# First convolution of a four-layer graph network: its first block ahead of all others, rows of x loaded in the third block, scores copied out of records by GpSimd

## The chip, the cores and the metric

The kernel runs on one core of one Trainium2 chip. The metric is the device time of one execution in microseconds (us), as the median of several runs. Lower is better. The core has five engines: TensorE (PE; PEld is its weight load), VectorE (DVE), ScalarE (ACT), GpSimd (POOL) and SyncE (SP), which only issues transfers. ACT and POOL issue transfers too, from the same in-order streams in which their computations stand.

## The reference

3125 nodes with 256 features x, 100,000 edges (src, dst) with 128 attributes and two weights each. Four graph layers follow one another; each adds its result to x and normalizes the rows.

```
edge_index = stack([src, dst])
x = layernorm(x + L0(x, edge_index, W1, W2))              # two graph convolutions
x = layernorm(x + L1(x, edge_index, edge_attr_128, ...))  # attention over edges
x = layernorm(x + L2(x, src, dst, edge_weight, ...))      # gated step, sums both ways
x = layernorm(x + L3(x, edge_index, W_conv, ...))         # convolution and decoder
```

The change lies in L0. With self-loops added to the edges, and deg the number of edges that end in a node:

```
gcn_conv(x, W): h = x @ W;  dinv = rsqrt(deg)
                return segment_sum(h[src] * (dinv[src] * dinv[dst])[:, None], dst)
L0(x) = gcn_conv(relu(gcn_conv(x, W1)), W2)
```

The score of an edge in L1 is a sum of a part from its source node and a part from its attributes. The latter, called q here, depends on the inputs alone.

## The kernel before

**Blocks and slabs.** The nodes lie in 25 blocks of 128 rows (`NBK`, `P`). Between two blocks lies a 128x128 count matrix; the 25 such matrices that end in one target block are its slab. A convolution is, for each target block, 75 matrix products that accumulate into one bank: 25 source blocks times three bf16 parts of each float32 feature (`apply_parts`, line 769, result `acc`).

**First stage (0 to 1041 us).** Chunks of 16 edges per partition are sorted into a table in device memory: a rank is computed for each edge, and POOL scatters its record (packed row numbers, the two weights, q) by an indirect transfer, 784 in all (line 498, `table`). ACT and DVE meanwhile make `H0`, the three bf16 parts of x @ W1 times dinv. The last of these parts come from lines 341 (ACT) and 343 (DVE, named `features` in the profile). The order of PE, DVE, ACT and SP in this stage is written out by hand (`manual_schedule`).

**First convolution (1041 to 1344 us).** This is the loop `for b in range(NBK)` from line 822. For each target block b:

- `load_records(b)`: SP loads the 50 columns of records of this block (line 803, `rec_b`, three buffers); it waits for all scatters. DVE unpacks the row numbers into `keys` and `keyd` (lines 807 to 814, five instructions), and ACT copies field 3 of the records into `q` (line 815).
- For the two halves of the slab (13 and 12 source blocks), DVE makes one-hot matrices: `os`, 128 columns, and `od`, 64 columns (line 723; two buffers each).
- `build_slab`: PE multiplies them (line 749, `slab`, three buffers, four source blocks in each), and ACT copies each group into the slab (line 750, `wo`, four buffers). The block's own matrix gets the identity on top, for the self-loops.
- SP stores the slab for later layers (line 829), PE applies it to `H0` (line 769), ACT applies relu and scale (line 832), PE turns the result and multiplies it with W2 (lines 680 and 687), and ACT and DVE split the product into three bf16 parts, `H1` (lines 706 to 710).

**What else is loaded here.** The rows of x, 3.2 MB, are issued by ACT at line 657, ahead of the loop. W2 is loaded by ACT ahead of the loop (line 820, through `weight`, line 666). The attention layer's `WnT`, `bn` and `attn_r` are loaded by ACT behind the loop in the text (lines 850 and 851; issues at lines 666 and 671). x is first read in the loop behind this one (line 877, the second convolution), WnT, bn and attn_r there as well.

**What sets the order.** Outside the first stage a planner orders the instructions of each engine. It ranks them by their place in the text, takes those that are ready by its own estimate of times, and so mixes stages and blocks: issues that stand behind the loop in the text can be placed ahead of it, and records of several blocks are loaded and unpacked far ahead. Each engine then runs its instructions strictly in that order. Line 648 adds a dependence by hand: `up` (line 647) comes behind the last of the parts (line 343).

**A second path** (`general_path`), for graphs that don't fit the slabs, stands behind a flag and doesn't run with these inputs.

Of the kernel before, what the change touches and what calls it, by code (L numbers as in the profile page):

```python
# [8 lines left out]
F32 = mybir.dt.float32  # L9
BF = mybir.dt.bfloat16  # L10
I32 = mybir.dt.int32
AF = mybir.ActivationFunctionType
# [6 lines left out]
P = 128  # L19
# [7 lines left out]
def row_bcast(vec, parts=P):  # L27

    return bass.AP(tensor=vec.tensor, offset=vec.offset, ap=[[0, parts], [1, vec.shape[0]]])
# [8 lines left out]
NBK = 25  # L38
# [3 lines left out]
TB = 2  # L42
HP = 64
# [9 lines left out]
KD = ND // P  # L53
# [46 lines left out]
def dense_path(ctx: ExitStack, tc: tile.TileContext, a: dict, out: bass.AP, flag: bass.AP):  # L100
    nc = tc.nc
    N, D = 3125, ND
# [548 lines left out]
    keyd = keep.tile([P, NT, 2], BF, name="keyd")  # L651
    keys = keep.tile([P, NT, 2], BF, name="keys")
# [1 line left out]
    nc.gpsimd.memset(x1[:, :, 0], 1.0)  # L654
    nc.gpsimd.memset(x1[:, :, D + 1], 1.0)
    x = x1[:, :, 1:D + 1]
    nc.scalar.dma_start(x, a["x_rows"])
    stats = keep.tile([P, NBK, 2], F32, name="stats")
    rstd = keep.tile([P, NBK], F32, name="rstd")
    s1 = keep.tile([P, NBK], F32, name="s1")  # L660


    def weight(pool, v, name):
        k, m = v.shape
        t = pool.tile([P, k // P, m], F32, name=name)
        nc.scalar.dma_start(t, v.rearrange("(k p) m -> p k m", p=P))
        return t

    def bias(pool, v, name):
        t = pool.tile([P, v.shape[0]], F32, name=name)  # L670
        nc.scalar.dma_start(t, row_bcast(v))
        return t
# [31 lines left out]
    def split(dst, src, shape):  # L704

        nc.scalar.activation(dst[0], src, AF.Copy)  # L706
        r = wk.tile(shape, F32, name="split")
        nc.vector.tensor_tensor(r, src, dst[0], op=OP.subtract)
        nc.scalar.activation(dst[1], r, AF.Copy)
        nc.vector.tensor_tensor(dst[2], r, dst[1], op=OP.subtract)  # L710
# [3 lines left out]
    def halfslab(name, bufs=2, cols=P):  # L714
        t = oh.tile([P, HALF[0] * TB, P], BF, name=name, tag=name, bufs=bufs)
        return t if cols == P else t.rearrange("p t (h c) -> p (t h) c", c=cols)
# [4 lines left out]
    def onehot(k, n, name, cols=P):  # L721
        t = halfslab(name, cols=cols)
        nc.vector.tensor_tensor(in_pairs(t[:, :n, :]), repeat(iota_b[:, :cols], n), pair(k, cols), op=OP.is_equal)  # L723
        return t

    def half_slabs():
        o = 0
        for n in HALF:
            yield o, n
            o += n  # L730

    def cut(k, b, o, n):

        return k[:, (b * NBK + o) * TB:(b * NBK + o + n) * TB, :]

    def build_slab(dst, b, o, n, stat, movs, self_loops=False):


        for g in range(0, n, 4):
            w = min(4, n - g)  # L740
            p = psB.tile([P, 4, P], F32, name="slab")
            for i in range(g, g + w):
                for j in range(TB):
                    own = slice(j * HP, (j + 1) * HP)
                    terms = [(stat[:, i * TB + j, :], mov[:, i * TB + j, :]) for mov in movs]
                    if self_loops and o + i == b:
                        terms.append((ident_b, ident_b[:, own]))
                    for m, (l, r) in enumerate(terms):
                        nc.tensor.matmul(p[:, i - g, own], l, r, start=(m == 0), stop=(m == len(terms) - 1))  # L749
            nc.scalar.activation(dst[:, g:g + w, :], p[:, :w, :], AF.Copy)  # L750
# [49 lines left out]
    def load_records(b):  # L800
        ts = slice(b * TS, (b + 1) * TS)
        r = wk.tile([P, TS, 4], F32, name="rec_b", bufs=3)
        load = nc.sync.dma_start(r, trows[:, ts, :])
        for name in done:
            tc.add_manual_dep(load.ins, name, DATA, reason="it reads rows of all scatters")
        both = wk.tile([P, TS], I32, name="both")
        nc.vector.tensor_copy(both, r[:, :, 0])
        for k, shift in ((keys, True), (keyd, False)):
            t = wk.tile([P, TS], I32, name="half")
            if shift:  # L810
                nc.vector.tensor_scalar(t, both, 8, None, op0=OP.arith_shift_right)
            else:
                nc.vector.tensor_scalar(t, both, HP - 1, None, op0=OP.bitwise_and)
            nc.vector.tensor_copy(k[:, ts, :], t[:, :, None].to_broadcast([P, TS, 2]))
        nc.scalar.activation(q[:, ts], r[:, :, 3], AF.Copy)


    s1p = keep.tile([P, NBK, 3], BF, name="s1p")
    with tc.tile_pool(name="layer0", bufs=1) as pool:
        W2 = weight(pool, a["L0_gnn_W2"], "W2")  # L820
        H1 = pool.tile([P, NBK, 3, D], BF, name="H1")
        for b in range(NBK):
            load_records(b)
            slab = halfslab("wo", 4)[:, :NBK, :]
            for o, n in half_slabs():
                os = onehot(cut(keys, b, o, n), n * TB, "os")
                od = onehot(cut(keyd, b, o, n), n * TB, "od", HP)
                build_slab(slab[:, o:o + n, :], b, o, n, os, [od], True)
            nc.sync.dma_start(slabs[b].rearrange("p (s d) -> p s d", d=P), slab)
            p = apply_parts(slab, H0, D)  # L830
            y = wk.tile([P, D], F32, name="tmp")
            nc.scalar.activation(y, p, AF.Relu, scale=dinv[:, b:b + 1])
            p = project(y, W2, D)
            h = wk.tile([P, D], F32, name="tmp2")
            nc.scalar.activation(h, p, AF.Copy, scale=dinv[:, b:b + 1])
            split([H1[:, b, i, :] for i in range(3)], h, [P, D])


        by_tile = keys.rearrange("p (n j) two -> p j n two", j=TB)
        rows_by_tile = rows.rearrange("(s j d) c -> j d s c", s=NBK, j=TB)  # L840
        for j in range(TB):
            for d in range(0, NBK, 5):
                p = psT.tile([P, P], BF, name="tp")
                nc.tensor.transpose(p[:5 * NBK, :], by_tile[:, j, d * NBK:(d + 5) * NBK, 0], ident_b)
                y = pool.tile([P, P], BF, name="rowt", bufs=2)
                nc.scalar.activation(y[:5 * NBK], p[:5 * NBK, :], AF.Copy)
                nc.scalar.dma_start(rows_by_tile[j, d:d + 5], y[:5 * NBK])


        WnT, bn = weight(pool, a["WnT"], "WnT"), bias(pool, a["L1_gnn_bn"], "bn")  # L850
        attn_r = bias(pool, a["L1_gnn_attn"].rearrange("o h c -> (o h c)"), "attn_r")
        H = features([P, NBK, D + 1], F32)
        nc.gpsimd.memset(H[:, :, D:], 1.0)
        q_by_source = q.rearrange("p (d s j) -> p s j d", d=NBK, j=TB)

        def scores(s):

            look = psL.tile([P, TS, 3], F32, name="look")
            for (o, n), tag in zip(half_slabs(), ("os", "od")):
                r = halfslab(tag)  # L860
                v = r.rearrange("p t c -> p (t c)")[:, :n * TB * P]
                nc.sync.dma_start(v, row_bcast(rows[s * TS + o * TB:s * TS + (o + n) * TB, :].rearrange("t c -> (t c)")))
                nc.vector.tensor_scalar(v, v, iota_p, None, op0=OP.is_equal)
                for t in range(n * TB):
                    nc.tensor.matmul(look[:, o * TB + t, :], r[:, t, :], s1p[:, s, :], start=True, stop=True,  # L865
                                     skip_group_check=True)
            sc = pool.tile([P, TS], F32, name="sc", bufs=2)
            nc.vector.tensor_reduce(sc, look, axis=AX.X, op=OP.add)
            qs = q_by_source[:, s]
            nc.vector.tensor_tensor(qs, qs, sc.rearrange("p (j d) -> p j d", j=TB), op=OP.add)  # L870
            nc.vector.scalar_tensor_tensor(qs, qs, 0.01, qs, op0=OP.mult, op1=OP.max)

        for b in range(NBK):
            p = apply_parts(load_slab(b), H1, D)
            if b:
                scores(b - 1)
            nc.vector.scalar_tensor_tensor(x[:, b, :], p, dinv[:, b:b + 1], x[:, b, :], op0=OP.mult, op1=OP.add)
            norm(b)
            p = project(x[:, b, :], WnT, D)
            nc.vector.tensor_add(H[:, b, :D], p, bn)  # L880
            m = wk.tile([P, D], F32, name="tmp")
            nc.vector.tensor_tensor(m, H[:, b, :D], attn_r, op=OP.mult)
            nc.vector.tensor_reduce(s1[:, b:b + 1], m, axis=AX.X, op=OP.add)
            nc.vector.tensor_scalar(s1[:, b:b + 1], s1[:, b:b + 1], kc, None, op0=OP.add)
            split([s1p[:, b, i:i + 1] for i in range(3)], s1[:, b:b + 1], [P, 1])
        scores(NBK - 1)
# [33 lines left out]
    with tc.tile_pool(name="layer1", bufs=2) as pool:  # L920
# [14 lines left out]
        r = largest(bmax, NBK)  # L935
# [854 lines left out]
```

## Time and profile before

| What | us |
|---|---|
| median of 10 runs (3315.73 to 3321.53) | 3319.2 |
| profiled execution, its own time | 3320.62 |
| its span | 3318.7 |

The stages of the profiled execution, from the windows view (busy time of each engine in us, and the granted TensorE clock as a share of full speed):

| Stretch, us | Stage | PE | DVE | ACT | POOL | Clock |
|---|---|---|---|---|---|---|
| 0 to 1041 | sorting, x @ W1 | 407 | 761 | 269 | 767 | 0.60 |
| 1041 to 1344 | first convolution | 284 | 168 | 130 | 0.2 | 0.96 |
| 1344 to 1642 | second convolution, scores | 280 | 157 | 30 | 0.1 | 0.97 |
| 1642 to 2066 | attention | 406 | 354 | 107 | 0 | 0.97 |
| 2066 to 3120 | gated step, both ways | 1039 | 680 | 357 | 21 | 1.00 |
| 3120 to 3319 | last convolution, decoder | 167 | 67 | 36 | 0 | 0.96 |

A row of the timeline or of the chain names the line of the kernel, the engine, the tile written, and the tile read (`wo<-slab`). A queue's own instructions have a q behind the engine's name (ACTq, SPq): issues of transfers and waits on semaphores. In brackets stands the time for which the engine was idle before an instruction, and what ended it. The chain of waits is followed back from the end of the program: at each step it names the work that released the next.

### The profile page before, as it was taken

The numbers are of one execution on the slowest core, as the hardware profiler recorded it, in microseconds if no ns is written. First come the engines' busy times: TensorE is split into PE (matmuls) and PEld (weight loads), VectorE is DVE, ScalarE is ACT, GpSimd is POOL, SyncE is SP. The second block draws the span as 40 slices with busy tenths as digits, with TensorE's granted clock in tenths as the row PEclk, the third lists the DMA queues.
The fourth block names the chain that finished last, engine by engine and source line by source line (L and its number), as shares of the span: only waits on it lengthen the run. The fifth ranks groups of instructions, "written<-read, shape, count | busy, mean of one in ns | idle before, by whom it ended". The sixth has DMA issues, their size and how long they took to land.

```text
span 3318.7 us, 62597 instructions
## 1 busy us (share of the span) xinstructions
PE 2582.0 (78%) x27062; PEld 2012.1 (61%) x27062; DVE 2186.4 (66%) x3751; ACT 928.7 (28%) x1851; POOL 788.3 (24%) x876
## 2 busy tenths in 40 slices
PE   4544333334422999999799999999999999999987
PEld 2222222222212888788688888888887676676676
DVE  8997766666773655355588888667666566566333
ACT  3222222222221444100122222222223333343311
POOL 4777777777774000000000000000000000000000
PEclk6555666666555999999899999999999999999999
DMA  4222222221203211565300000000011001000242
GB/s 136 82 78 64 70 70 74 76 71 57 78 17 90 86 71 71 209 232 210 119 2 2 2 2 30 20 16 16 16 15 14 11 10 11 11 10 7 73 135 90
DMA packets 171999, 203.63 MB, mean 61 GB/s; under 512 B 119719, under 2 KB 144796, under 8 KB 165441
## 3 DMA queue, kind: packets, MB, share of 16 engines
q1 hardware_dynamic: 132438, 186.72, 17.2%
q10 hardware_dynamic: 14187, 11.17, 1.2%
q0 software_dynamic: 25088, 1.66, 0.8%
q8 instruction: 213, 3.49, 0.4%
q14 instruction: 73, 0.60, 0.1%
HBM read 167.60 MB, written 31.86 MB: 60 GB/s over the span
## 4 chain that ended last, share of the span: by engine, by line
PE 48%; DVE 20%; POOL 18%; issue 8%; ACT 4%; DMA 2%; ACTq 1%; DVEq 0%; POOLq 0%; SPq 0%
POOL table L498 17%; PE acc L777 17%; PE acc L769 12%; PE mm L687 7%; PE slab L749 5%; DVE wo L903 4%; DVE os L723 3%; PE tp L680 2%; DVE eq L465 1%; PE slab L761 1%; PE look L865 1%; ACT xT L681 1%; DVE rank L469 1%; DVE st L696 1%; DVE od L723 1%
## 5 line engine op out<-in xcount | busy, mean ns | idle before, releaser
L498 POOL DMA_INDIRECT table<-rec,row x784 | 756.4, 965 | 261.5 <-issue 218.1
L777 PE MATMUL acc<-x,slab_f 128*128 128x257 f32 x2500 | 592.6, 386 | 0.0
L903 DVE TENSOR_TENSOR wo<-od,w 128x1664 bf16<-128x1664 bf16 (+1 forms) x450 | 435.1, 986 | 131.7 <-PE slab L749 107.9
L769 PEld LDWEIGHTS <-wo 128*128 128x128 bf16 x5625 | 476.3, 99 | 61.7 <-issue 9.8
L777 PEld LDWEIGHTS acc<-x,slab_f 128*128 128x128 f32 x2500 | 455.9, 189 | 71.4 <-issue 5.7
L361 PE MATMUL place<-by_target,op 128*128 128x100 bf16 x392 | 40.7, 281 | 464.0 <-ACT tick L512 413.5
L749 PEld LDWEIGHTS <-os 128*128 128x128 bf16 x8750 | 296.6, 98 | 108.1 <-issue 83.4
L723 DVE TENSOR_TENSOR os<-iota_b,keys 128x3328 bf16<-128x3328 bf16 (+1 forms) x150 | 273.0, 1820 | 115.3 <-PE slab L749 114.2
L769 PE MATMUL acc<-H,wo 128*128 128x256 bf16 (+1 forms) x3750 | 342.5, 247 | 1.2 <-ACT H L706 0.8
L361 PEld LDWEIGHTS <-op 128*128 128x128 bf16 x392 | 33.6, 135 | 467.0 <-issue 281.9
L777 PE MATMUL acc<-features,slab_f 128*128 128x257 f32 x1250 | 297.2, 388 | 0.0
L749 PE MATMUL slab<-wo,os 128*128 128x64 bf16 x7500 | 261.0, 193 | 13.4 <-ACT slab_f L750 8.2
L777 PEld LDWEIGHTS acc<-features,slab_f 128*128 128x128 f32 x1250 | 227.9, 190 | 43.3 <-issue 12.1
L750 ACT ACTIVATE slab_f<-slab 128x512 f32<-128x512 f32 (+1 forms) x350 | 182.4, 549 | 146.1 <-PE slab L749 138.4
L769 PE MATMUL acc<-features,wo 128*128 128x256 bf16 x1875 | 213.7, 274 | 0.0
L1032 POOL COPY keys_t<-keys 128x2500 bf16<-128x2500 bf16 x1 | 2.5, 2522 | 721.8 <-ACT tmp L969 721.8
L512 ACT ACTIVATE tick<-place 1x1 f32<-1x1 f32 x48 | 7.7, 160 | 530.0 <-POOL tock L513 497.6
L465 DVE TENSOR_SCALAR eq<-gap 128x512 bf16<-128x512 f32 x196 | 121.8, 683 | 40.8 <-PE gap L439 40.8
L723 DVE TENSOR_TENSOR od<-iota_b,keyd 128x1664 bf16<-128x1664 bf16 (+1 forms) x150 | 147.9, 986 | 0.0
L1111 DVE TENSOR_TENSOR gate<-mm,bx 128x512 f32<-128x512 f32 x25 | 17.3, 691 | 190.9 <-PE mm L687 190.9
L687 PE MATMUL mm<-features,xT 128*128 128x512 f32 x300 | 135.7, 593 | 0.0
L761 PEld LDWEIGHTS <-wo 128*64 128x64 bf16 x3750 | 108.5, 110 | 43.8 <-issue 43.8
(289 smaller groups left out, 3497.9 us busy)
## 6 DMA issues: line engine op xcount, KB each, us to landing
ea<-in_edge_attr SPq DMA_DIRECT2D x49, 1024.0 KB
wo<-slabs SPq DMA_DIRECT2D x50, 800.0 KB
os<-rows SPq DMA_DIRECT2D x25, 832.0 KB
slabs<-wo SPq DMA_DIRECT2D x25, 800.0 KB
od<-rows SPq DMA_DIRECT2D x25, 768.0 KB
table<-rec,row POOLq DMA_INDIRECT x784
dr<-db_row SPq DMA_DIRECT2D x48, 208.0 KB
rec_b<-table SPq DMA_DIRECT2D x75, 100.0 KB
```

The source lines that it names most:

```text
L361: nc.tensor.matmul(deg, op[:, c:c + 2, :], od[:, c:c + 2, :TS], start=(c == 0), stop=(c == CH - 2), skip_group_check=True)
L465: nc.vector.tensor_scalar(eq[:, 4 * g:4 * g + 4, :], of[k]["gap"][g], 0.0, None, op0=OP.is_equal)
L498: i = nc.gpsimd.indirect_dma_start(out=table, out_offset=bass.IndirectOffsetOnAxis(ap=ready[k][:, c:c + 1], axis=0), in_=rec[:, k * CH + c ...
L680: nc.tensor.transpose(p[:, j, :], srcs[i + j], ident)
L687: nc.tensor.matmul(p[:, :m], l, r, start=(i == 0), stop=(i == len(w) - 1))
L723: nc.vector.tensor_tensor(in_pairs(t[:, :n, :]), repeat(iota_b[:, :cols], n), pair(k, cols), op=OP.is_equal)
L749: nc.tensor.matmul(p[:, i - g, own], l, r, start=(m == 0), stop=(m == len(terms) - 1))
L750: nc.scalar.activation(dst[:, g:g + w, :], p[:, :w, :], AF.Copy)
L761: nc.tensor.matmul(p[j * HP:(j + 1) * HP, i - g, :], stat[:, i * TB + j, :], mov[:, i * TB + j, :], start=(m == 0), stop=(m == len(stats) ...
L769: nc.tensor.matmul(p[:, :m], slab[:, s, :], parts[:, s, k, :m], start=(s == 0 and k == 0), stop=(s == NBK - 1 and k == 2))
L777: nc.tensor.matmul(p[:, :m], t[:, s, :], H[:, o + s, :m], start=(o + s == 0), stop=(o + s == NBK - 1))
L903: nc.vector.tensor_tensor(in_pairs(t[:, :n, :]), in_pairs(oh[:, :n, :]), pair(w3[k], HP), op=OP.mult)
```

## The change

Four things are edited, all in the dense path:

- The first block's `load_records`, one-hots and slab (b = 0) are ranked ahead of everything else that is ready, by a priority of 20,000 places.
- The load of x leaves its place ahead of the loop. At the end of the loop's third pass (b = 2), ACT issues x, WnT, bn and attn_r in this order. Each is pinned behind the ACT instruction that stands before it in the text; other ACT instructions, of later blocks too, may still be placed ahead of them.
- W2 is loaded by SP instead of ACT, behind the first block's slab in the text.
- q is copied out of the records by POOL (`tensor_copy`) instead of ACT (`activation`).

```diff
-    nc.scalar.dma_start(x, a["x_rows"])
...
-    def weight(pool, v, name):
+    def weight(pool, v, name, q=nc.scalar):
         k, m = v.shape
         t = pool.tile([P, k // P, m], F32, name=name)
-        nc.scalar.dma_start(t, v.rearrange("(k p) m -> p k m", p=P))
+        q.dma_start(t, v.rearrange("(k p) m -> p k m", p=P))
         return t
...
-        nc.scalar.activation(q[:, ts], r[:, :, 3], AF.Copy)
+        nc.gpsimd.tensor_copy(q[:, ts], r[:, :, 3])
...
     with tc.tile_pool(name="layer0", bufs=1) as pool:
-        W2 = weight(pool, a["L0_gnn_W2"], "W2")
         H1 = pool.tile([P, NBK, 3, D], BF, name="H1")
         for b in range(NBK):
-            load_records(b)
-            slab = halfslab("wo", 4)[:, :NBK, :]
-            for o, n in half_slabs():
-                os = onehot(cut(keys, b, o, n), n * TB, "os")
-                od = onehot(cut(keyd, b, o, n), n * TB, "od", HP)
-                build_slab(slab[:, o:o + n, :], b, o, n, os, [od], True)
+            with tc.high_priority(0 if b else 20000):
+                load_records(b)
+                slab = halfslab("wo", 4)[:, :NBK, :]
+                for o, n in half_slabs():
+                    os = onehot(cut(keys, b, o, n), n * TB, "os")
+                    od = onehot(cut(keyd, b, o, n), n * TB, "od", HP)
+                    build_slab(slab[:, o:o + n, :], b, o, n, os, [od], True)
+            if b == 0:
+                W2 = weight(pool, a["L0_gnn_W2"], "W2", nc.sync)
             nc.sync.dma_start(slabs[b].rearrange("p (s d) -> p s d", d=P), slab)
             p = apply_parts(slab, H0, D)
...
             split([H1[:, b, i, :] for i in range(3)], h, [P, D])
+
+            if b == 2:
+                WnT = pool.tile([P, KD, D], F32, name="WnT")
+                bn, attn_r = [pool.tile([P, D], F32, name=n) for n in ("bn", "attn_r")]
+                for t, v in ((x, a["x_rows"]), (WnT, a["WnT"].rearrange("(k p) m -> p k m", p=P)), (bn, row_bcast(a["L1_gnn_bn"])),
+                             (attn_r, row_bcast(a["L1_gnn_attn"].rearrange("o h c -> (o h c)")))):
+                    tc.keep_in_program_order(nc.scalar.dma_start(t, v))
...
-        WnT, bn = weight(pool, a["WnT"], "WnT"), bias(pool, a["L1_gnn_bn"], "bn")
-        attn_r = bias(pool, a["L1_gnn_attn"].rearrange("o h c -> (o h c)"), "attn_r")
```

## The prediction

> **What bounds the kernel now.** I read the page's slices first. TensorE (PE) is busy nine tenths of the time from about 1060 us on, and before that the clock granted to it is about half. The chain of waits, cut to 1000 to 1100 us, says why the seam at 1040 us matters:
>
> ```profile
> 1038.49 2.10 DMA table<-rec,row
> ...
> 1041.43 13.82 DMA x<-in_x_rows
> 1055.27 0.35 ACTq L671
> ...
> 1056.44 0.49 ACT wo L750
> ...
> 1059.37 9.54 PE acc L769 x71
> ```
>
> The columns are start, length and what ran. The last scattered record lands at 1040.6. From there the chain is not computation but the load of x: ScalarE's queue stands at `bn` (line 671) until x has landed, and the first slab copy (line 750) stands behind it. The timeline of the same stretch (start, length, engine, line, what; in brackets the idle time before and what ended it):
>
> ```profile
> 1040.92 9.79 SPq L803 DMA_DIRECT2D rec_b<-table  x6
> 1042.17 0.42 ACT L341 ACTIVATE features<-xs 128x256 bf16<-128x256 f32 x1 [42.30 <-issue]
> 1043.45 0.20 DVE L807 CAST both<-rec_b 128x50 int32<-128x50 f32 x1 [43.13 <-DMA rec_b<-table]
> 1047.45 0.20 DVE L807 CAST both<-rec_b 128x50 int32<-128x50 f32 x1 [2.50 <-DMA rec_b<-table]
> 1048.16 0.42 DVE L343 TENSOR_TENSOR features<-xs,features 128x256 bf16<-128x256 f32 x1
> 1048.69 1.89 DVE L723 TENSOR_TENSOR os<-iota_b,keys 128x3328 bf16<-128x3328 bf16 x1
> 1050.57 1.02 DVE L723 TENSOR_TENSOR od<-iota_b,keyd 128x1664 bf16<-128x1664 bf16 x1
> 1051.64 0.21 PE L749 MATMUL slab<-od,os 128*128 128x64 bf16 x1 [62.15 <-DVE od L723]
> 1053.31 0.95 DVE L723 TENSOR_TENSOR od<-iota_b,keyd 128x1536 bf16<-128x1536 bf16 x1
> 1056.35 0.58 ACT L750 ACTIVATE wo<-slab 128x512 bf16<-128x512 f32 x1
> 1057.89 1.49 PE L749 MATMUL slab<-od,os 128*128 128x64 bf16 x24
> ```
>
> Two delays stand one behind the other. VectorE (DVE) has block 0's records at 1043.45, but decodes those of blocks 0, 1 and 2 and waits 2.5 us for the third before the first one-hot at 1048.69. PE then fills its three slab buffers and stops at about 1053.2, because ScalarE (ACT) copies nothing out until 1056.35. From 1057 PE hardly stops again: in the windows view it is busy 12.00 of 12.00, 11.62 of 12.00, 11.38 of 12.00 and 11.37 of 11.50 us up to 1104.5. What starts PE earlier at this seam is therefore taken off the end.
>
> **The change, part by part.** All shifts are taken at one event: the start of block 0's second half of slab products, 1057.89 before.
>
> 1. Block 0 first on DVE. The records still land at 1043.45 (nothing ahead of that load changes). Five decodes at a pitch of 0.12 us (1043.45 to 1044.16, read off the timeline) end at 1044.16 instead of three sets of five and a wait. The one-hots then follow at their own pitch: os 1.80 (block 1: 1057.28 to 1059.08), od 0.94, os 1.67, od 0.95. So the first od ends at 1047.0 and the second at 1049.5, against 1051.59 and 1054.26: 4.6 and 4.7 us earlier. Behind them, later than now, come the decodes of blocks 1 and 2 (1.4 us) and line 343 (0.42); block 1's one-hots then take 5.4 us from about 1051.9 and are there at 1057.3, before PE has finished block 0 (below, about 1060), so that is hidden. Without that cover it would cost up to its 1.8 us.
>
> 2. The load of x leaves ACT's queue here, with WnT, bn and attn_r (0.69, 0.40, 0.35 and 0.46 us of issue), and W2 (0.41) goes to SP's queue behind block 0's records. ACT is free when the first slab group is done, 1047.6, so PE need not stop: four groups of eight products, three buffers, one copy in 0.58. Line 341, which stood 42.3 us behind x's issue, runs at 1000.4. PE starts the second half when its one-hots are there, 1049.6 instead of 1057.9: **8.3 us earlier**. It is both parts together; the freed queue alone would give the stop of 3.8 us. W2 is next needed at the first `mm` (1070.40 now, about 1061 then); even behind line 343 it has over 8 us, and a 256 KB load cannot take what x's 3.2 MB took.
>
> 3. PE's clock. It goes to full 5.9 us after the steady start, as the windows of half a microsecond show (busy time of PE, PEld, DVE, ACT and POOL, then the granted clock, here 0.62 on its way from 0.50 to 1.00, the DMA share and GB/s):
>
> ```profile
> 1062.50:1063.00 0.50, 0.50 (x5) 0.35 (x4) 0.50 (x5) 0.00 (x0) 0.00 (x0) 0.62 0.99 397
> ```
>
> Of the 71 products from 1059.37 about 17 ran at 0.215 and 54 at 0.109 us (together 9.54). Counted from PE's first product at 1047.0, full clock comes at 1052.9; from the second half at 1049.6, at 1055.4. The tail then takes 8.7 or 9.9 us: from +0.9 to -0.4. I take +0.3, the middle. [...]
>
> 4. The copies of q go from ACT (25 of 0.29 us, line 815) to GpSimd (POOL). No copy of this shape on POOL is in the trace. From below: `tock`, 0.19; from above: 2500 elements in 2.52, line 1032. I take 0.3, nearest to 50 elements. POOL has nothing else after 1041.6, so their own time is hidden; SP's loads of records wait for them as they waited for ACT's. What can hurt is DVE:
>
> ```profile
> 2066.58 2.52 POOL L1032 COPY keys_t<-keys 128x2500 bf16<-128x2500 bf16 x1 [721.78 <-ACT tmp L969]
> 2068.31 0.93 DVE L702 TENSOR_SCALAR x<-x,stats,rstd 128x256 f32<-128x256 f32 x1
> ```
>
> Line 702 takes 0.41 elsewhere; here it ends just behind POOL's copy, 0.5 longer. So a copy can hold DVE. In the five critical microseconds only three copies fall (three record buffers): 0 to 0.9 us; I take -0.3. The other 22 meet a DVE busy 0.55 of this stage. [...]
>
> 5. ACT without q. Blocks 1 and 2 take 12.0 and 11.7 us (1072.07, 1084.07, 1095.74) where later ones take 11.45; at 1092.29 a q copy that waited for its records runs just ahead of line 832, for which PE waits. 0 to +0.7; I take +0.3.
>
> 6. Line 343 and `up` may come before block 0's one-hots, as now: 0 to -0.6. I take -0.2, since ACT hands line 343 its operand 40 us earlier and DVE idles then.
>
> 7. The four issues in block 2: 1.9 us on ACT behind the last copy of block 2's split (1097.19 now). ACT idles 6.23 us there, until the products of block 3 end, so 0; -1.9 if that cover is gone. x is first read at 1355.8; 3.2 MB in about 14 us beside slab stores of 0.8 MB in 11.5 us is hidden by over 200 us.
>
> Sum: 8.3 + 0.3 - 0.3 + 0.3 - 0.2 = **8.4 us**. The profiled execution took 3320.62 (span 3318.7 and 1.9 around it) and would take 3312.2; it stands 1.4 above the median of the ten runs, 3319.2, so the forecast is 3310.8.
>
> **The rivals.**
>
> *bn waits for x again* (slower). Place: ACT, block 2, behind x's issue. The list of waits has issues that wait for transfers whose data they do not touch:
>
> ```profile
> ACT q L815 <- DMA x<-in_x_rows: 6.4, 1, 6.4
> ```
>
> ```profile
> SPq L162 <- DMA attn<-in_L_gnn_attn: 4.0, 1, 4.0
> ```
>
> If WnT, bn or attn_r is held until x lands, ACT stands 13.8 us, and some 2 more because a slab store runs beside it, while 6.2 are covered. PE loses 7.6 to 9.6, and, if its clock falls, some 3 more (6 us at half speed, part 3). That leaves 3310.8 plus 7.6 to 13, 3318 to 3324; it decides once ACT is held over 14.6 us (6.2 + 8.4). Against it: W2 and WnT, the first two issues behind x, did not wait for it; only the third, with loads of SP between, did. In the new order attn_r is the third, close behind. Held on SP instead, x costs nothing: records are ten blocks ahead and four slab buffers allow 40 us.
>
> *Half of it only* (no change that counts). Something else is late once x is gone: records of block 0, the order on DVE as now, or POOL's copies. Only the stop of 3.8 us goes: 3315.4. For it: rows 1047.45 to 1048.62 show how the planner mixes blocks. Against: DVE idles 43 us, so nothing must precede block 0.
>
> *Given back at the next seam.* At 1344 to 1380 PE idles several microseconds behind small row stores. If that wait ends at a fixed transfer time the shift passes on; I see no wait there on a clock of its own, and leave up to 2 us of it in the range.
>
> **How the numbers follow.** Forecast 0.70, own range 3307.5 to 3313.5 (sum of the ends: 8.3+0.9+0.7 against 8.3-0.4-0.9-0.6-0.7, widened by 2 for the next seam on one side and run scatter on the other). Half only 0.17. bn waits 0.13. Two tenths of a per cent, 6.6 us, is about what a measurement of this kernel can tell from no change: 3312.6 and 3325.8. Of the forecast nine tenths lie below 3312.6: faster 0.64. Slower is the far end of the rival, where the clock falls and more is held: 0.09. Same 0.27. The range 3306.5 to 3317.5 holds the forecast and half of it, and leaves out the rival.
>
> **What would show it.** The first one-hot near 1044.2, the first slab copy near 1047.8, the second half near 1049.6, full clock between 1052 and 1056, block 3's products within 0.5 us of 8.3 us earlier. Wrong if ACT shows an idle time ended by x in blocks 2 to 3, if DVE decodes blocks 1 and 2 first, or if the one-hots grow beyond 1.9 us beside POOL's copies.

## The result, and the profile after

The changed kernel took 3341.97 us (median of 8 runs, 3339.69 to 3343.53), against 3318.52 for the kernel before on the same chip (28 runs, 3314.64 to 3321.53). The ratio is 1.0071, with a 95% interval of 1.0062 to 1.0079: 23 us slower, where 8.4 us faster was forecast.

The seam, the passage from the sorting stage into the loop, did what was forecast and a little more. The loss came behind it, in the loop. The table cuts the profiled executions at two events: the start of the last scatter, and block 0's relu (`tmp<-acc,dinv`, line 832 before, 833 after). From there the loop is 24 periods from one relu to the next.

| us | before | after | difference |
|---|---|---|---|
| start of the last scatter | 1038.49 | 1039.23 | +0.7 |
| seam: to block 0's relu | 30.44 | 20.33 | -10.1 |
| periods of blocks 1 and 2 | 11.65, 11.91 | 12.72, 12.25 | +1.4 |
| period of block 3 | 11.37 | 22.23 | +10.9 |
| 21 later periods, mean | 11.47 | 12.40 | +19.7 |
| behind the loop, to the end of the span | 1974.07 | 1974.12 | 0 |
| span | 3318.7 | 3341.3 | +22.6 |

The seam in the timeline of the kernel after (start, length, engine, line, what; in brackets the idle time before and what ended it):

```profile
1043.82 0.20 DVE L806 CAST both<-rec_b 128x50 int32<-128x50 f32 x1 [1.37 <-DMA rec_b<-table]
...
1044.65 1.89 DVE L722 TENSOR_TENSOR os<-iota_b,keys 128x3328 bf16<-128x3328 bf16 x1
1044.88 2.81 POOL L814 COPY q<-rec_b 128x50 f32<-128x50 f32 x2 [0.48 <-DMA rec_b<-table]
1046.46 1.09 DVE L722 TENSOR_TENSOR od<-iota_b,keyd 128x1664 bf16<-128x1664 bf16 x1
...
1048.39 1.75 ACT L749 ACTIVATE wo<-slab 128x512 bf16<-128x512 f32 x4 [46.89 <-PE slab L748]
...
1050.23 0.98 PE L748 MATMUL slab<-od,os 128*128 128x64 bf16 x15 [0.28 <-DVE od L722]
```

The first one-hot follows block 0's five decodes at once, ACT copies as soon as PE has filled a buffer, and PE's second half starts at 1050.23 instead of 1057.89.

Two things are new behind it. The first is in the list of the costliest groups (line, operation, count, busy time and mean in ns, then the idle time before the group and what ended it). Before and after:

```profile
L769 PE MATMUL acc<-features,wo 128*128 128x256 bf16 x1875 | 213.7, 274 | 0.0
```

```profile
L768 PE MATMUL acc<-features,wo 128*128 128x256 bf16 x1875 | 224.6, 275 | 23.4 <-ACT wo L749 23.4
```

The products with the features, which did not wait before, now wait 23.4 us for ACT's slab copies, 7.3 of them in block 3. The second is a piece of ACT's timeline in block 3:

```profile
1088.56 0.68 ACTq L844 DMA_DIRECT2D x<-in_x_rows  x1
1089.28 6.02 ACTq L844 DMA_DIRECT2D WnT<-in_WnT  x1
...
1095.34 0.71 ACTq L844 DMA_DIRECT2D bn<-in_L_gnn_bn  x1
1096.09 0.44 ACTq L844 DMA_DIRECT2D attn_r<-in_L_gnn_attn  x1
1096.58 1.25 ACT L749 ACTIVATE wo<-slab 128x512 bf16<-128x512 f32 x3 [7.61 <-issue]
1097.23 5.77 PE L768 MATMUL acc<-features,wo 128*128 128x256 bf16 x27 [7.32 <-ACT wo L749]
```

The issue of WnT, 0.40 us before, holds ACT for 6.02. PE stands 7.32 us, and the 27 products behind it take 5.77 instead of some 3.1, since the granted clock fell meanwhile (windows view: stretch, length, busy time of PE, PEld, DVE, ACT and POOL, granted clock, DMA share, GB/s):

```profile
1088.00:1090.00 2.00, 1.91 (x28) 1.63 (x26) 1.14 (x3) 0.48 (x2) 0.00 (x0) 1.00 0.04 8
...
1092.00:1094.00 2.00, 0.00 (x0) 0.00 (x0) 0.54 (x1) 0.00 (x0) 0.00 (x0) 0.61 1.09 373
1094.00:1096.00 2.00, 0.00 (x0) 0.00 (x0) 0.00 (x0) 0.00 (x0) 0.00 (x0) 0.50 1.10 350
...
1098.00:1100.00 2.00, 2.00 (x12) 1.39 (x10) 0.00 (x0) 0.00 (x0) 0.00 (x0) 0.50 1.10 349
```

Data still moved at 350 GB/s when WnT's issue ended at 1095.3. The rates of the windows up to there add up to about 1.7 MB, so about half of x's 3.2 MB had gone by then (an estimate).

Why do the products wait for copies in every block? The order of the instructions on PE, as the traces have it, for one block before (from 1172.6 us on) and for two blocks after (from about 1189 on). The number is the count of products; `slab` builds a slab, `acc` applies one, `tp` and `mm` turn and multiply the result:

```
before  slab 15, tp 2, slab 13, mm 4, slab 24, acc 75
after   acc 36, slab 15, tp 2, slab 6, acc 3, mm 4, acc 21, slab 15, acc 27, slab 24,
        acc 29, tp 2, acc 4, mm 4, acc 3, slab 20, acc 27, slab 24
```

Before, PE builds a whole slab, while ACT copies it out, and then applies one with 75 products in one run. After, building and applying are mixed: PE fills slab buffers and soon has to apply what ACT has not copied yet. So PE waits for ACT about twice a block (47 waits in all), as its timeline shows:

```profile
1210.13 3.12 PE L768 MATMUL acc<-features,wo 128*128 128x256 bf16 x27 [0.59 <-ACT wo L749]
1213.09 0.86 PE L748 MATMUL slab<-od,os 128*128 128x64 bf16 x24
1214.18 4.11 PE L768 MATMUL acc<-features,wo 128*128 128x256 bf16 x36 [0.22 <-ACT wo L749]
```

### The profile page after: what moved, and what is told of

Same layout as the page of the kernel before. It is cut to its first block, busy times and chain, and to the rows that moved or that the text cites. A ratio compares the mean times of both kernels' runs of the same rounds, so it can differ in the third digit from the quotient of the medians.

```text
span 3341.3 us, 62598 instructions
## 1 busy us (share of the span) xinstructions
PE 2606.7 (78%) x27062; PEld 2015.9 (60%) x27062; DVE 2189.8 (66%) x3751; ACT 931.2 (28%) x1826; POOL 803.8 (24%) x901
## 4 chain that ended last, share of the span: by engine, by line
PE 48%; DVE 19%; POOL 18%; issue 8%; ACT 5%; DMA 2%; ACTq 1%; DVEq 0%; SPq 0%; POOLq 0%
POOL table L498 17%; PE acc L776 17%; PE acc L768 12%; PE mm L686 7%; PE slab L748 5%; DVE wo L909 4%; DVE os L722 3%; PE tp L679 2%; PE slab L760 1%; DVE eq L465 1%; PE look L871 1%; DVE st L695 1%; DMA table<-rec,row 1%; ACT wo L749 1%; DVE od L722 1%
## 5 line engine op out<-in xcount | busy, mean ns | idle before, releaser
L768 PE MATMUL acc<-features,wo 128*128 128x256 bf16 x1875 | 224.6, 275 | 23.4 <-ACT wo L749 23.4
L420 PEld LDWEIGHTS <-by_target 128*52 128x52 bf16 x784 | 90.1, 137 | 77.3 <-issue 49.0
```

The lines of the kernel that those rows point to most:

```text
L420: nc.tensor.matmul(cnt[:, c + 1:, :], it["by_target"][:, c], it["by_source"][:, c:c + 1, :].to_broadcast([P, CH - c, KB]), start=False, st ...
L768: nc.tensor.matmul(p[:, :m], slab[:, s, :], parts[:, s, k, :m], start=(s == 0 and k == 0), stop=(s == NBK - 1 and k == 2))
```

## The experiments

The theory after these readings: the slow loop comes from the priority context, the long block 3 from an issue held because x stands ahead of it, the gain at the seam from x's absence. Rivals: the gain needs the first block's rank, as the prediction had it; the loop is slow because of what x's move or POOL's copies do to ACT and the transfers; within the context, block 0's 20,000 places are what disturbs the order. Runs e5 to e8 went to a second chip and e9 to e12 to a third. The sorting stage takes about 150 us longer on both. Each ratio is to the kernel before on the same chip; where the loop or the seam of such a run is compared with the kernel before, that kernel's profile is the one of the first chip.

### One part at a time

**e1: the priority context alone**, put into the kernel before.

```diff
-            load_records(b)
-            ...
+            with tc.high_priority(0 if b else 20000):
+                load_records(b)
+                ...
```

> The kernel before with the priority of block 0 alone; x, W2 and q stay on ScalarE as before. Theory: the priority makes the planner set another order for the whole loop (products of block b start before its slab is complete), and that costs about 0.94 us in each of some 24 blocks. ScalarE still stands until x has landed, so nothing is gained at the seam: 3318.5 + 20 to 23 = 3338 to 3342, with TensorE idle before acc and wo as what ended it. Rival (the load of x in block 2 or the copies on GpSimd are the whole loss): none of them is here, 3316 to 3320.

Measured: 3339.21 us, ratio 1.006 [1.0046, 1.0074]. The later periods are 12.26 and 12.57 in turn, as after; the whole loop takes 298.27 us against 275.70, +22.6. The products' group shows the waits:

```profile
L769 PE MATMUL acc<-features,wo 128*128 128x256 bf16 x1875 | 223.0, 274 | 16.9 <-ACT wo L750 16.9
```

The waits are 16.9 of the 22.6 us; the rest is in no row shown here.

And the seam gained nothing: 31.16 us against 30.44. The timeline of e1 says why:

```profile
1049.21 0.42 DVE L343 TENSOR_TENSOR features<-xs,features 128x256 bf16<-128x256 f32 x1
...
1049.72 1.89 DVE L723 TENSOR_TENSOR os<-iota_b,keys 128x3328 bf16<-128x3328 bf16 x1
...
1055.62 0.35 ACTq L671 DMA_DIRECT2D attn_r<-in_L_gnn_attn  x1
```

Block 0's one-hot still stands right behind line 343, and DVE still decodes three blocks first. ACT is held to 1055.62 as before.

**e2: the move of x, WnT, bn and attn_r alone.**

```diff
-    nc.scalar.dma_start(x, a["x_rows"])
...
+            if b == 2:
+                ...
+                    tc.keep_in_program_order(nc.scalar.dma_start(t, v))
```

> The kernel before with the four loads (x, WnT, bn, attn_r) moved to the third pass alone; no priority, W2 and q on ScalarE. Theory: the order of the loop stays as before, 11.5 us a block; at the seam ScalarE is free, 3.6 to 6 us earlier; the issue of WnT is held 6 us behind x as after, but most of it lies in the 6.2 us in which ScalarE idles, so it costs 1 to 3: 3313 to 3317. Rival (the held issue, not the order, is the loss): 3325 to 3341.

Measured: 3312.44 us, ratio 0.9981 [0.9972, 0.999], just under the 3313 to 3317 expected. The seam took 20.83 us, nearly the whole of the gain:

```profile
1000.29 0.42 DVE L343 TENSOR_TENSOR features<-xs,features 128x256 bf16<-128x256 f32 x1 [0.48 <-ACT features L341]
...
1042.66 0.20 DVE L806 CAST both<-rec_b 128x50 int32<-128x50 f32 x1 [1.45 <-DMA rec_b<-table]
...
1043.42 1.89 DVE L722 TENSOR_TENSOR os<-iota_b,keys 128x3328 bf16<-128x3328 bf16 x1
```

Line 343 needs the result of line 341 on ACT, which in the kernel before stood 42.3 us behind x's issue. With x gone it runs at 1000.3, and block 0's one-hot follows its decodes with no priority at all. WnT's issue is held here too, 7.57 us, but in the old order of the loop most of it falls into ACT's idle time of 6.2 us: block 3 takes 14.55 us, 3.0 more than its neighbours.

**e3: q on POOL alone** (`nc.gpsimd.tensor_copy(q[:, ts], r[:, :, 3])`).

> The kernel before with q copied by GpSimd alone. Theory: 0 to 0.7 us off, 3317.5 to 3319, loop at 11.45 to 11.5 us a block. Rival (GpSimd's copies hold VectorE in the loop): blocks 1 to 3 longer than 11.9 us, 3320 to 3330.

Measured: 3314.43 us, ratio 0.9987 [0.9978, 0.9996]: 4.1 us faster, more than the 0 to 0.7 expected. The seam took 26.34 us, since ACT is not held at `bn`:

```profile
1049.61 0.54 ACTq L671 DMA_DIRECT2D bn<-in_L_gnn_bn  x1
...
1052.49 1.75 ACT L750 ACTIVATE wo<-slab 128x512 bf16<-128x512 f32 x4 [10.77 <-PE slab L749]
```

In the kernel before, `bn` was issued at 1055.27, when x had landed; in e1 it was `attn_r` that stood so long. Which issue is held until x lands thus changes with edits elsewhere; what decides it was not tried. The first three periods of the loop are 11.39, 11.39 and 11.38, against 11.65, 11.91 and 11.37, so blocks 1 and 2 gain 0.8 us besides.

**e4: the kernel after without the context.**

> The changed kernel without the priority; x in the third pass, W2 by SP and q by GpSimd stay. Theory: loop at 11.5 us a block, block 0's first one-hot still behind the records of blocks 1 and 2, ScalarE free: 3312 to 3317. Rival (the order is not set by the priority but by the moved loads or copies): loop at 12.4 us, 3330 to 3342.

Measured: 3313.49 us, ratio 0.9984 [0.9975, 0.9993]. The seam stays at 20.25 us, the later periods go back to 11.49, and blocks 3 and 4 take 14.17 and 13.24: the held issue (6.12 us here) costs 4.5. Part of this is the clock: PE stops for 2.59 us in block 3, and the granted clock is 0.50 from 1098.6 to 1102.0, which makes block 4 long: four products of `mm` take 1.51 us from 1098.01 on (1.13 in the next block), and 74 with the features 8.86 (8.09 in e2). Taking the context out of the changed kernel gives back 28 us: the 22.6 of e1, and the part of the hold that falls into ACT's idle time in the old order. W2's move was not tried alone; e2 and e4, which differ by it and by q, differ by 0.6 us at the seam.

### What in the context

The context wraps all 25 blocks, with an offset of 20,000 places for block 0 and of 0 for the others. Either could mix the loop.

**e9: the context on block 0 only** (kernel after, `with tc.high_priority(20000) if b == 0 else ExitStack():`).

> The changed kernel with the priority context around block 0 alone; the other 24 blocks stand in no context instead of one with offset 0. Theory: the context sets the planner's count of places back when it ends, so with offset 0 the slab and the products of a block get equal ranks; that, and not block 0's rank, mixes them in the 24 later blocks. Then blocks take 11.45 to 11.5 us again, the seam keeps its 10 us, the held issue costs about 4.5 as in the run without priority: 3311 to 3315 beside 3318.5 for before. Rival (block 0's rank sets another rhythm that lasts): 12.4 us a block, 3338 to 3342.

Measured: ratio 0.9981 [0.9964, 0.9997], later periods 11.45 us. WnT's issue held ACT 5.97 us, and blocks 3 and 4 took 13.98 and 11.61 (+2.6). PE stopped for 2.40 us in block 3, about as long as in e4, but here the clock stayed at 1.00: the 74 products behind it took 8.09 us. The seam takes 20.46 us, as in e4 without any context, so ranking block 0 first adds nothing there once x is gone.

**e10: offset 0 on every block**, in the kernel before (`with tc.high_priority(0):`), and nothing else.

> The kernel before with the context of offset 0 around every block's records, one-hots and slab, block 0's too, and nothing else changed. Theory: nobody is ranked ahead, yet the loop takes about 12.4 us a block: 3337 to 3342 beside 3318.5 for before. Rival (an offset of 0 does nothing): 3317 to 3320.

Measured: ratio 1.0058 [1.0038, 1.0077], periods 12.26 and 12.57, loop +22.2 us. The first line is e9's group of products, the second e10's:

```profile
L768 PE MATMUL acc<-features,wo 128*128 128x256 bf16 x1875 | 212.1, 273 | 0.0
```

```profile
L769 PE MATMUL acc<-features,wo 128*128 128x256 bf16 x1875 | 223.5, 274 | 21.8 <-ACT wo L750 21.6
```

The context with offset 0 is the cause, and the 20,000 places are not. My reading is that the planner's count of places is set back when the context is left: the products behind it then get the same ranks as the slab building inside it, and the planner takes both in turn. The order on PE fits that; no run looks inside the planner.

**e6: the order restored by hand.** Kernel after, and each later block's first product pinned behind what stands before it in the text:

```diff
+                if pin and s == 0 and k == 0:
+                    tc.keep_in_program_order(i)
```

> The changed kernel with the first product of each block from block 1 on pinned on TensorE behind the last slab product of that block, so that the planner has to keep the order of before. Theory: blocks at 11.45 to 11.5 us; the 9.4 us of the seam stay; the held issue falls mostly into ScalarE's idle 6.2 us and costs 1.5 to 3: 3310 to 3313. Rival (the blocks are longer because GpSimd's copies or the transfers disturb the engines): blocks above 12 us, 3330 to 3342.

Measured: ratio 0.9989 [0.9976, 1.0002]; later periods 11.49 to 11.55, and the products wait for nothing:

```profile
L768 PE MATMUL acc<-features,wo 128*128 128x256 bf16 x1875 | 210.5, 274 | 0.0
```

It is the order of PE that costs the loop its 20 us, since here the context stays and only the order goes back. The held issue (6.24 us) costs blocks 3 and 4 4.4 us (14.04, 13.32), more than the 1.5 to 3 expected: as in e4 the clock is 0.50 for 3.4 us (1259.4 to 1262.8), behind a stop of PE of 2.36 us, and 75 products take 9.32 us (8.20 in the next block).

**e8: the same pin in the kernel before.**

> A control: the kernel before with the same pin and nothing else. Its order is nearly that of before, so 3317 to 3319.5 by every theory; if the pin by itself gains or loses more than 1 us, the run with the pin in the changed kernel must be read against this one.

Measured: ratio 1.0003 [0.9987, 1.0019], loop 277.16 us (the last 12 periods take 11.55 instead of 11.45). The pin by itself gains nothing, so e6 is not faster than the kernel after for the pin's own sake.

### The held issue

Is it x's place ahead of WnT, and does it depend on how much of x is outstanding?

**e5: the kernel after with x as the last of the four issues** (the tuple in the order WnT, bn, attn_r, x).

> The changed kernel with x issued as the last of the four loads instead of the first. Theory: WnT's issue is held because x's 3200 rows stand ahead of it in the same queue; behind nothing long no issue is held, block 3 takes about 12.4 us instead of 22.2, so 9 to 10 us off the changed kernel: 3331 to 3333. Rival (ScalarE is held by any issue in this place, or by a wait on x as data): 3340 to 3343.

Measured: ratio 1.0058 [1.0039, 1.0077]. WnT's issue takes 0.40 us and x's own 0.68:

```profile
1252.53 0.40 ACTq L844 DMA_DIRECT2D WnT<-in_WnT  x1
...
1254.12 0.68 ACTq L844 DMA_DIRECT2D x<-in_x_rows  x1
```

Block 3 takes 13.88 us instead of 22.23; 12.4 was expected, so the four issues by themselves still cost about 1.5 in the mixed order. The loop goes from 307.62 to 299.35: the hold was worth 8.3 us there. The ratio alone would not show it, since its interval holds the 1.0071 of the kernel after; the time is above the one expected, the issue and block 3 decide. The rest of the loss stays, as it must.

**e7: pin and x last together.**

> Both: the pinned order, and x issued last of the four. Theory: seam gain of 9.4 and nothing given back, 3308 to 3310, 1.5 to 3 us below the pinned order alone. Rival (the held issue is hidden in the pinned order): the same as the pinned order alone.

Measured: ratio 0.998 [0.9966, 0.9995]; blocks 3 and 4 take 11.50 and 11.68, and the loop 276.78. With both causes taken out, 1 us of the loop's 32 is left. By time alone the intervals of e6 and e7 are not apart.

**e11: no context, x last.**

> The changed kernel without any priority context and with x issued last of the four loads. Theory: the seam's 10 us stay, blocks at 11.45 to 11.5, no held issue: 11 to 13 us below before, 3305.5 to 3308 beside 3318.5. Rival (the held issue is mostly hidden in this order): as the run without priority, 3312 to 3315.

Measured: ratio 0.9972 [0.9952, 0.9991]; 3467.71 us against 3475.23. The seam takes 21.61 us, the loop 275.06. That is 7.5 us faster by the medians (9.5 in the sum of seam and loop, against the kernel before on the first chip), a little short of what was expected. Block 3 takes 11.39 us: no issue is held.

**e12: no context, x in two loads**: columns 0 to 11 of each partition (12 of 25 blocks), WnT, bn, attn_r, then the rest.

```diff
-                for t, v in ((x, a["x_rows"]), (WnT, ...), (bn, ...), (attn_r, ...)):
+                for t, v in ((x[:, :12], a["x_rows"][:, :12]), (WnT, ...), (bn, ...), (attn_r, ...),
+                             (x[:, 12:], a["x_rows"][:, 12:])):
```

> The changed kernel without priority, and x in two loads: 1536 rows first, then WnT, bn and attn_r, then the other 1664 rows. Theory (the queue has room for a limited number of rows, so an issue is held only until about half of x's 3200 rows have moved): no issue of the first four is held over 1 us, the second half of x at most a little: 3306 to 3309 beside 3318.5. Rival (an issue behind any long transfer of the same queue is held until a share of it has moved): WnT held about 3 us, 3309 to 3313.

Measured: ratio 0.9965 [0.9946, 0.9983], 3466.31 us.

```profile
1250.23 0.40 ACTq L843 DMA_DIRECT2D x<-in_x_rows  x1
1250.67 1.57 ACTq L843 DMA_DIRECT2D WnT<-in_WnT  x1
```

Behind 1536 rows of 1 KB WnT's issue takes 1.57 us, behind 3200 rows 6.0 to 7.6. It is neither the free 0.4 nor a wait for x to land: 1.57 MB in the 2 us since x's issue began would be more than twice the 350 GB/s of the kernel after. The hold is longer behind the longer load, but its rule stays open: the limited room for rows that was expected gave under 1 us, the rival's share of the transfer about 3, and no run shows either. Block 3 takes 11.39: 1.57 is covered.

e11 and e12 beat the kernel before, and by far the kernel after; the intervals don't tell them from each other, nor from e2, e4, e7 and e9. No run tries the four loads on SP's queue.

## Why the prediction was wrong

**The sum of the loss.** Seam -10.1 (table), mixed order +22.6 (e1's loop against the kernel before), held issue and the rest of the loop +9.3 (307.62 - 298.27), scatters 0.7 later: +22.5, and the span grew by 22.6. The last two are a split by differences between runs. The prediction's sum had the first term and neither of the other two; something like the third stood among its rivals.

**Step 1, block 0 first, is where it failed most.** It read the context as an edit of block 0 alone and priced what moves there. The other 24 blocks are inside the same context, with offset 0, and I counted that as no edit; e10 shows that this offset alone costs 22 us. The diff showed it; what it does to the order of a block's building and its products was never asked. Nor did I ask what holds the order of the loop together, although the profile before had it: 75 products in one run of 8.35 us, with no wait for a copy.

The step's own times held. From the last scatter, the second half started 8.4 us earlier (7.66, and the scatter was 0.74 later), against 8.3.

**Steps 1 and 2 had the right size from the wrong part.** "The freed queue alone would give the stop of 3.8 us" is refuted: x's move alone gave 9.6 (e2), the context alone -0.7 (e1). I took the decodes of blocks 1 and 2 for a matter of rank. They left their place when x's issue went (e2), not when block 0 was ranked first (e1). In DVE's order block 0's one-hot stood behind line 343, line 343 needs line 341, and that stood behind x's issue. The row of line 341 with its 42.30 us of idle time was quoted, and not followed to line 343 and the one-hot behind it. In the run itself line 341 was done at 1042.59, before block 0's records came, so the time went to the order and not to a late operand. That the planner reckoned with a late operand and filled the wait with decodes is my reading; no run tests it. The 8.3 came out because the whole change held what the step had undervalued, x's move.

**Step 3, the clock.** Forecast +0.3, measured about +1.7 (10.1 - 8.4): full clock was granted from 1051.5, ahead of the 1052 to 1056 named, so all of the 72 last products ran at 0.111 us (8.02). That is 3.9 us after PE's first product at 1047.61, where the step carried over 5.9 us, the distance from PE's restart at 1056.97 in the kernel before. The distance isn't fixed: it is about 5.1 us in e2 and 3.1 in e4 (estimates from the times of the products behind it; e2's 72 took 8.66). So some of the 1.7 is chance; from the second half to the relu it takes 10.0 us in e2, 9.3 after and 9.0 in e4. In windows of 0.1 us the clock of the kernel after rises at 1051.50, falls at 1092.46 and rises again at 1102.70; the distances, 40.96 and 10.24 us, are 12 and 3 times the 3.41 us of the shortest stretches at one clock in the same trace (177.69 to 181.10 is one). The fall came 2.6 us after PE stopped at 1089.9. The length of a stop does not decide alone: with stops of 2.4 to 2.6 us the clock fell in e4 and e6 and not in e2 and e9 (behind the stop 74 products took 8.86 us in e4 and 75 took 9.32 in e6, against 8.09 for 74 in both others).

**Step 4, POOL's copies.** Forecast -0.3 for DVE. The first os took 1.89 us as elsewhere and od 1.09 (1.02 before): 0.07 more, as much as for block 0's second os (1.82 against 1.75). What was held was POOL: two copies in 2.81 us beside the one-hots (from 1044.88, behind the one-hot's start at 1044.65), and 0.27 to 0.40 each for the nine from 1058.7 to 1065.5, when no one-hot ran. So here POOL paid for nearly all of it, and only SP's loads waited for POOL, 0.6 us in all.

**Step 5, ACT without q.** Forecast +0.3, from blocks 1 and 2. In e3 these two gain 0.8, and the seam gains 4.1 more through the issue of `bn`, which the step did not look at. In the changed kernel the latter is inside the seam's gain, as the issue is gone there, and the former is lost in the mixed order.

**Step 6** came out as +0.2 against the forecast: line 343 ran 40 us earlier and cost nothing at the seam.

**Step 7, the four issues, failed.** It priced them at 1.9 us from rows in which WnT stood 7.8 us behind x's issue (1041.43 to 1049.19), and took that as covered. Put 0.7 us behind it, WnT's issue took 6.0 to 7.6 us. The cover of 6.23 us that it named was real, and in the old order took most of it: blocks 3 and 4 lost 2.6 to 4.5 us together, the more where the clock fell (e4 and e6: 4.5 and 4.4; e2 and e9: 3.2 and 2.6). In the mixed order it was gone, and the hold cost 8.3 (e5 against the kernel after).

**The rivals.** *bn waits for x again* had the right place, ACT behind x's issue, and the right kind of loss, with the clock falling. Its mechanism was off: it was the first issue behind x and not the third, it was held for about half of x and not until it landed, and for 6 us instead of 13.8. Alone it would not have turned the sign (e4: 0.9984). *Half of it only* is refuted by e2 and e4. *Given back at the next seam*: nothing was (1974.07 against 1974.12 behind the loop). The loss that decided the sign, an order of the loop in which PE waits for ACT, was in no rival.

## What to carry to other kernels

A planner's order is part of a tuned kernel: price an edit of ranks for every instruction inside it, those with a neutral-looking offset too, and compare the order as built before any time is forecast. Try to load small tensors ahead of a large one on the same queue, or to cut the large one: here the engine that issues was held for 5.97 to 7.57 us (0.40 with the small load ahead), and computing instructions stood behind it. An order that looks like a free choice (three decodes before the first one-hot) can hang on another instruction's place: here it changed when x's issue went. Follow what stands between two instructions back to what it needs.

## What the runs showed of the hardware

- An issue on ACT's queue right behind a load of 3200 rows of 1 KB took 5.97 to 7.57 us in the five kernels that have it there (after, e2, e4, e6, e9); behind 1536 rows 1.57; ahead of the load 0.40. The load's own issue took 0.68 or 0.69.
- POOL's copy of 128x50 took 0.27 to 0.40 us while no one-hot ran on DVE (after, 1058.7 to 1065.5), and about 1.4 beside one-hots (after two in 2.81, in e3 three in 4.73), whose larger form took 1.89 there, and 1.96 once in e3.
- Behind a stop of PE of 7.3 us the clock was 0.50 (after, 1092.46 to 1102.70), and 27 products took 5.77 us instead of 3.12. Of four runs with stops of 2.4 to 2.6 us, e4 and e6 show slower products behind it (74 in 8.86 and 75 in 9.32 us), e2 and e9 don't (74 in 8.09). Rises and falls lay 40.96 and 10.24 us apart in the kernel after, 12 and 3 times the 3.41 us of the shortest stretches at one clock.
- On the second and third chip the sorting stage was some 150 us longer with the same scatters (0.96 us each in e5); the loop periods of kernels of the same order agreed with the first chip's within 0.1 us.
